# Output projection of seven query groups as seven block products in one step, and the second layer's mask held per group

## The chip, the cores and the metric

The kernel runs on one core of a Trainium2 chip. The metric is the device time of one execution in microseconds (us), lower is better. The profile is one execution taken by the hardware profiler; its times count from the first instruction. The engines are named as in the profile: PE (matrix multiply; PEld is its weight load), DVE (vector), ACT (scalar, activation functions), POOL (GpSimd) and SP (which issues most DMAs). PE writes to PSUM, the small accumulation memory, which DVE and ACT read[...]; everything else lies in SBUF.

## The reference

Two graph layers, each added to its input and normalised, on 4096 nodes with 512 features. The first is a graph attention with 4 heads over a given 0/1 adjacency. The second, which is where the change lies, is a masked attention with 8 heads of width 64:

```python
adj = jnp.maximum(adjacency_matrix, eye)
q = jnp.einsum('nd,hdk->hnk', node_matrix, Wqs)
k = jnp.einsum('nd,hdk->hnk', node_matrix, Wks)
v = jnp.einsum('nd,hdk->hnk', node_matrix, Wvs)
scores = jnp.einsum('hqk,hmk->hqm', q, k) * kd ** (-0.5)
scores = scores + IDENTITY_BIAS * eye - MASK_VAL * (1.0 - adj)
att = jax.nn.softmax(scores, axis=-1)
return jnp.einsum('hqm,hmk,hko->qo', att, v, Wo)
...
x = _layernorm(x + _L1_gnn_ref(...), axis=-1)
```

All inputs and the output are float32. The last einsum contains the output projection: the heads' outputs side by side, 4096 x 512, times Wo, 512 x 512.

## The kernel before

The first layer and the products for q, k and v fill the first 1455 us or so. They already use block products of the kind that the change brings to the output projection: a 2 x 2 blocking in which seven products of sums of blocks stand for eight (`of_weights`, `of_features`, `order`, `gemm`).

The second layer's attention follows, to the end. Queries are cut into NG = 8 groups `g` of G = 512; heads go in four pairs `m` (0 to 3). One (g, m) is called a pair here; there are 32, in the order of `pairs`. In a pair, the keys are walked in 32 tiles `j` of 128; (g, m, j) is a unit. For each unit:

- `score` (L1067): PE multiplies k and q into a PSUM tile `s_ps` of 128 keys x 2 heads x 512 queries. The pool `ps` has three such tiles, used in turn.
- `weigh` (L1281, L1284): ACT takes the exponential in place; DVE multiplies it with the mask (`keep`) into an SBUF tile `p1`, of which there are 18. The mask is float8; the 4 key tiles that hold the group's diagonal use `mdt` instead, a float32 copy made by ACT (L1044) whose diagonal POOL sets (`affine_select`, L1046).
- `add_up`: the sums over keys that the softmax divides by. Two neighbouring `p1` tiles are added by a DMA that POOL issues (L1314) and that accumulates; POOL then adds the result to `q_sum` (L1304). Two of sixteen times POOL adds both tiles itself.
- `products` (L1329): PE multiplies v and `p1` and accumulates over the 32 units in the PSUM tile `o1_ps`.

The order is written out by hand; every engine works through its instructions in program order. `step` takes a batch of NB = 3 units. It issues the scores of the batch, then its weighing and adding up, and then the products of the batch before. A pair has eleven steps, numbered 0 to 10 in this text; the last has only two units, and takes in what is left over: the row sums of the pair before (`half_sums`, L1348), and from the sixth pair on the projection of one tile of 128 queries of the group before (`project`, L1393). Both use a third `s_ps` tile, `extra`. `Later` keeps small work for later steps: `later.at(n, fn)` runs `fn` at the end of the n-th step, the current one counted as the first. So `divide` puts off the reciprocals (DVE, L1371), their spreading (ACT, L1363) and the multiplication that gives `on`, the normalised attention output of the pair (POOL, L1367, six steps on).

`project` multiplies `on` of four head pairs with `wo_sb`, four matmuls of 128 x 128 with 128 x 512. In the profile every float32 matmul shows as two records. `close1` (L1403) adds the residual `y`, which `load_y` brought, and takes the mean and variance (`normal_factors`: DVE, then four small POOL operations); four steps later ACT normalises and SP stores the rows. Four pairs of a group thus carry the four tiles of the group before. After the last pair a tail does what is left: DVE adds up the last `p1` tiles (L1461), PE projects the last five tiles, and so on.

SP loads k and v in chunks of CH = 8 key tiles, one chunk ahead (`loads`, `load_kv`), q per pair, and the mask: `load_adjT` (L1034) takes 4 key tiles x W = 1024 queries, so two groups, as it lies in DRAM (4096 bytes a partition); eleven such tiles of 4 KB a partition are kept, and the next two groups' mask is loaded during m = 3 of every second group. The spare room for sums of blocks in the q, k and v products (`spare`) comes from the same tiles.

## Time and profile before

| what | value |
|---|---|
| time, median of 3 runs | 3380.09 us (3379.16 to 3389.31) |
| the profiled execution, first to last instruction (span) | 3376.2 us |
| PE busy | 3351.0 us, 99% of the span |
| DVE busy | 2405.8 us, 71% |
| ACT busy | 1991.2 us, 59% |
| POOL busy | 2244.8 us, 66% (95% or more in the second layer's attention) |
| DMA engines, mean rate | 184 GB/s |

The three run times are of unprofiled executions; of the profiled one only the span is known. A matmul's record is longer than the time for which it keeps the next one waiting, since matmuls are pipelined, so times on PE are read from start to start. A line such as "x24 ... 2.75" merges 24 records in a row. An engine's idle time ahead of an instruction is given in brackets with what ended it.

### The profile page before, as it was taken

What the parts mean: (1) busy time and instruction counts of PE and PEld (TensorE: products, weight loads), DVE (VectorE), ACT (ScalarE), POOL (GpSimd) and SP (SyncE); (2) the same over time, 40 slices, a digit from 0 to 9 for tenths busy, and PEclk for the clock granted to TensorE, in tenths of its full rate; (3) what the DMA queues carried; (4) which work ended last, traced back from release to release, by engine and by line L of the source; (5) the groups of instructions that cost most, each with busy time, mean ns of one, the idle gap of its engine ahead of it and who ended that gap; (6) DMA issues with size and microseconds to landing.
All of it is one profiled execution on the core that took longest, in us unless ns stands there. A gap on an engine that the chain in (4) does not pass through costs nothing.

```text
span 3376.2 us, 66035 instructions
## 1 busy us (share of the span) xinstructions
PE 3351.0 (99%) x26970; PEld 1921.4 (57%) x26970; DVE 2405.8 (71%) x2485; ACT 1991.2 (59%) x2468; POOL 2244.8 (66%) x1592
## 2 busy tenths in 40 slices
PE   9999999999999999999999999999999999999998
PEld 5669999999999855543333333333333333333332
DVE  6889899998898721157766767666676666667676
ACT  1347877878876421156665656656566656656564
POOL 5650021030030174569999999999999999999996
PEclk9999999999999999999999999999999999999999
DMA  7989979769451263388989898899989889898884
GB/s 192 202 157 159 183 195 213 172 141 210 132 163 64 42 210 111 115 223 193 211 193 223 223 212 194 201 207 233 215 190 211 195 199 254 192 211 192 205 198 111
DMA packets 397129, 620.36 MB, mean 184 GB/s; under 512 B 165520, under 2 KB 242576, under 8 KB 395792
## 3 DMA queue, kind: packets, MB, share of 16 engines
q0 software_dynamic: 97376, 258.50, 42.2%
q1 hardware_dynamic: 298912, 356.49, 35.4%
q8 instruction: 214, 3.51, 0.4%
q10 hardware_dynamic: 528, 1.05, 0.1%
q14 instruction: 99, 0.81, 0.1%
HBM read 315.87 MB, written 117.64 MB: 128 GB/s over the span
## 4 chain that ended last, share of the span: by engine, by line
PE 97%; DVE 1%; DMA 1%; ACT 0%; POOL 0%; issue 0%; SPq 0%; POOLq 0%; DVEq 0%
PE o_ps L1016 27%; PE o_ps L1329 26%; PE s_ps L1067 26%; PE s_ps L1132 5%; PE s_ps L1393 3%; PE o_ps L877 3%; PE s_ps L1125 3%; PE o_ps L818 2%; DMA wq<-in_L_gnn_Wqs_dram 1%; PE s_ps L1348 1%; PE o_ps L871 0%; PE x_ps L997 0%; PE x_ps L735 0%; DVE p L1461 0%; PE x_ps L1125 0%; DVE x_sb L784 0%
## 5 line engine op out<-in xcount | busy, mean ns | idle before, releaser
L1304 POOL TENSOR_TENSOR q_sum<-q_sum,p 128x1024 f32<-128x1024 f32 x538 | 1375.8, 2557 | 62.2 <-DMA p<-p 39.0
L1284 DVE TENSOR_TENSOR p<-s_ps,adjT 128x1024 f32<-128x1024 f32 x896 | 1043.7, 1216 | 466.2 <-ACT s_ps L1281 443.4
L1281 ACT ACTIVATE s_ps<-s_ps 128x1024 f32<-128x1024 f32 x1021 | 967.1, 1006 | 594.5 <-PE s_ps L1067 594.3
L1329 PE MATMUL o_ps<-p,v_sb 64*64 64x512 f32 x8192 | 943.6, 590 | 0.0
L1067 PE MATMUL s_ps<-q_sb,k_sb 64*64 64x512 f32 x8192 | 942.7, 589 | 0.0
L1016 PE MATMUL o_ps<-sup_t,p 128*128 128x129 f32 x8192 | 922.3, 275 | 3.9 <-DVE p L633 3.9
L1016 PEld LDWEIGHTS o_ps<-sup_t,p 128*128 128x128 f32 x8192 | 919.7, 192 | 4.9 <-DVE p L633 3.9
L633 DVE SCALAR_TENSOR_TENSOR p<-fr_t,dj,az 128x1024 f32<-128x1024 f32 x512 | 654.6, 1288 | 80.9 <-PE o_ps L1016 53.5
L1329 PEld LDWEIGHTS o_ps<-p,v_sb 64*64 64x64 f32 x8192 | 310.3, 133 | 570.6 <-issue 560.3
L1067 PEld LDWEIGHTS s_ps<-q_sb,k_sb 64*64 64x64 f32 x8192 | 312.8, 133 | 565.9 <-issue 457.0
L624 ACT ACTIVATE z<-fr_t,f 128x1024 fp8e4<-128x1024 f32 x512 | 558.0, 1144 | 120.1 <-DVE az L628 119.7
L1314 POOL DMA_DIRECT2D p<-p x412 | 438.3, 1303 | 10.0 <-PE o_ps L1329 8.4
L980 POOL DMA_DIRECT2D agg<-base_d x32 | 28.6, 1201 | 526.8 <-ACT agg L967 526.6
L1284 DVE TENSOR_TENSOR p<-s_ps,md 128x1024 f32<-128x1024 f32 x128 | 150.5, 1217 | 67.3 <-ACT s_ps L1281 63.4
L628 DVE TENSOR_TENSOR az<-adjT,z 128x512 int32<-128x512 int32 x256 | 176.0, 688 | 4.1 <-ACT z L624 3.4
L584 POOL COPY seen<-token 128x1 f32<-128x1 f32 x24 | 14.0, 582 | 240.1 <-DVE token L582 240.1
L1139 ACT ACTIVATE sb<-s_ps 128x1024 f32<-128x1024 f32 x35 | 35.8, 1024 | 188.6 <-PE s_ps L1132 125.9
L597 ACT ACTIVATE adjT<-stage 128x1024 fp8e4<-128x1024 bf16 x128 | 130.9, 1050 | 4.5 <-DMA stage<-adj_d 4.5
L1154 POOL TENSOR_TENSOR sb<-sb,sb 128x1024 f32<-128x1024 f32 x36 | 84.4, 2359 | 71.7 <-ACT sb L1139 71.7
L877 PE MATMUL o_ps<-pw_sb,xT 128*128 128x512 f32 x256 | 115.1, 592 | 0.0
L1178 DVE COPY k_sb<-s_ps 128x1024 f32<-128x1024 f32 x12 | 14.7, 1224 | 139.2 <-PE s_ps L1132 89.5
L1393 PE MATMUL s_ps<-wo_sb,on 128*128 128x512 f32 x240 | 110.8, 604 | 0.0
(164 smaller groups left out, 2171.7 us busy)
## 6 DMA issues: line engine op xcount, KB each, us to landing
p<-p POOLq DMA_DIRECT2D x412, 512.0 KB, 9.1
k_sb<-k_d SPq DMA_DIRECT2D x128, 512.0 KB, 8.0
v_sb<-v_d SPq DMA_DIRECT2D x128, 512.0 KB, 5.9
adj_d<-in_adj_dram POOLq DMA_DIRECT2D x32, 1024.0 KB, 12.3
sup_t<-sup_d SPq DMA_DIRECT2D x120, 258.0 KB, 7.3
fr_t<-fr_d SPq DMA_DIRECT2D x16, 1024.0 KB, 7.5
adjT_d<-adjT SPq DMA_DIRECT2D x32, 512.0 KB, 4.5
adjT<-adjT_d SPq DMA_DIRECT2D x32, 512.0 KB, 6.7
```

Of the source, the lines that this page charges most:

```text
L624: nc.scalar.activation(z[:, k, :], fr[:, 0, :], AF.Sign, bias=fs[j // GT][:, 0, (j + k) % GT, h:h + 1], saturate=False)
L628: nc.vector.tensor_tensor(az.bitcast(I32), adjT[w, j // CJ][:, j % CJ:j % CJ + 2, :].bitcast(I32), z.bitcast(I32), op=ALU.bitwise_and)
L633: nc.vector.scalar_tensor_tensor(p, fr[:, 1, :], dj[j // GT][:, j % GT, h:h + 1], az_t[w, h, j // 2][:, j % 2, :], op0=ALU.max, op1=ALU.mult)
L877: nc.tensor.matmul(b_ps, xT[:, c, t * P:(t + 1) * P], pw_sb[c], start=(c == 0), stop=(c == KC - 1))
L1016: nc.tensor.matmul(o[t // BK][:, t % BK, :], p[:, t * P:(t + 1) * P], s, start=(j == 0 and t % BK == 0), stop=(j == NT - 1), skip_group_ch ...
L1067: nc.tensor.matmul(s[c:c + MS, e, :], k[r, a + c:a + c + MS], qt[g, m][r, :], start=True, stop=True)
L1281: nc.scalar.activation(s, s, AF.Exp)
L1284: nc.vector.tensor_tensor(p, s, keep[:, None, :].to_broadcast([P, HP, G]), op=ALU.mult)
L1304: nc.gpsimd.tensor_tensor(q, q, p, op=ALU.add)
L1314: later.at(2, lambda: nc.gpsimd.dma_start(a, b, accum_op=ALU.add))
L1329: nc.tensor.matmul(o[c, n, :], v[r, j % CH, c], p[r, e, :], start=(j == 0), stop=(j == NT - 1))
L1393: nc.tensor.matmul(s, on_t[g][:, m, t * P:(t + 1) * P], wo_sb[:, m, :], start=(m == 0), stop=(m == NP1 - 1))
```

## The change

The projection of groups 0 to 6 no longer goes tile by tile. For each of them, one extra step in the pair (g + 1, 1) projects all 512 queries at once. `on` (512 queries x 512) and `wo` (512 x 512) are cut into 2 x 2 blocks of 256 x 256, and the result is built from seven products of blocks or sums of blocks instead of eight, in four PSUM banks; each product is four matmuls of 128 x 128 with 128 x 256. The last group is still projected tile by tile in the tail.

```diff
+            def combine_wo(i):
+                a, b = {5: (wo_block(0, 1), wo_block(0, 0)), 6: (wo_block(1, 1), wo_s[5]),
+                        7: (wo_block(1, 1), wo_block(0, 1)), 4: (wo_block(1, 0), wo_s[6])}[i]
+                nc.vector.tensor_tensor(wo_block(0, 1) if i == 7 else wo_s[i], a, b,
+                                        op=ALU.subtract)
...
+            def combine_on(g, i):
...
+                a, b, op = {5: (on_block(g, 1, 0), on_block(g, 1, 1), ALU.add),
+                            6: (on_s[5], on_block(g, 0, 0), ALU.subtract),
+                            7: (on_block(g, 0, 0), on_block(g, 1, 0), ALU.subtract),
+                            3: (on_block(g, 0, 1), on_s[6], ALU.subtract)}[i]
+                nc.vector.tensor_tensor(on_block(g, 1, 0) if i == 7 else on_s[i], a, b, op=op)
+
+            def project_group(g):
+                ts = [ps.tile([P, HP, G], F32, name="s_ps") for _ in range(2)]
...
+                def add(dst, src):
+                    nc.vector.tensor_tensor(dst, dst, src, op=ALU.add)
+
+                for i in (1, 5, 2, 6, 7, 3, 4):
+                    more = i in (2, 3, 4)
+                    for t in range(2):
+                        for c in range(2):
+                            nc.tensor.matmul(bank[i][:, t, :], a[i][:, c, t * P:(t + 1) * P],
+                                             b[i][:, c, :], start=not more and t == 0 and c == 0,
+                                             stop=c == 1, skip_group_check=True)
+                    if i == 1:
+                        nc.scalar.activation(u, bank[1], AF.Copy)
+                    elif i == 6:
+                        add(u, bank[6])
+                    else:
+                        add(y[{5: (1, 1), 2: (0, 0), 7: (1, 1), 3: (0, 1), 4: (1, 0)}[i]], bank[i])
+
+                add(y[0, 1], u)
+                for m in range(2):
+                    later.at(1, lambda m=m: add(y[1, m], u))
+                for t in range(GT):
+                    later.at(2 + t, lambda t=t: close1(g, t))
```

Products 2, 3 and 4 accumulate in the banks of 1, 5 and 7. The four sums of `wo` are made once, on DVE, one every second step from the end of step 8 of the second pair on; the fourth block is overwritten in place, and `load_wo_again` brings it back after pair (7, 1) for the last group. The four sums of `on` are made on DVE for each group.

The steps of a pair with a block are cut otherwise, twelve instead of eleven: eight of three units, then one unit (step 8, which has the block), three, two (with the row sums) and two. Two sums of `on` are issued ahead of step 6 and two ahead of step 7, before those steps' own work; the residual's two tiles (four DMAs) ahead of step 0:

```diff
+            with_block = cut([NB] * (n_full - 2) + [1, NB, 2, 2])
...
+                    if block is not None and k == 0:
+                        for i in range(2):
+                            load_y(block, i)
+                    if block is not None and k in (n_full - 4, n_full - 3):
+                        for i in ((5, 6), (7, 3))[k - n_full + 4]:
+                            combine_on(block, i)
```

In `step`, `project_group` stands after the weighing of the step's unit and before the products of the step before.

The mask is kept per group, in six tiles of 8 key tiles x 512 queries (4 KB a partition), each filled by two DMAs with runs of 512 bytes, and loaded during m = 3 of every group at key tiles 0, 12 and 20. The room for sums of blocks in the q, k and v products gets tiles of its own, except for three that still come from the mask's:

```diff
-        def load_adjT(w, c):
-            at[w, c] = lp.tile([P, CJ, W], F8, name="adjT1", bufs=NCJ + 3)
-            nc.sync.dma_start(at[w, c], adjT_d[w][c])
+        def load_mask(g, c):
+            at[g, c] = lp.tile([P, CH, G], F8, name="mask", bufs=NCH + 2)
+            r = g * G % W
+            for k in range(CH // CJ):
+                nc.sync.dma_start(at[g, c][:, k * CJ:(k + 1) * CJ, :],
+                                  adjT_d[g * G // W][c * CH // CJ + k][:, :, r:r + G])
...
-                if m == NP1 - 1 and (g + 1) * G % W == 0 and g + 1 < NG and j % CJ == 0:
-                    for c in ((0, 1) if j == 0 else (j // CJ + 1,) if j // CJ + 1 < NCJ else ()):
-                        load_adjT((g + 1) * G // W, c)
+                if m == NP1 - 1 and g + 1 < NG:
+                    for c in {0: (0, 1), CH + CJ: (2,), 2 * CH + CJ: (3,)}.get(j, ()):
+                        load_mask(g + 1, c)
```

## The prediction

> **What bounds the kernel now.** I read the page first: busy shares, then the chain that ended last (97% PE). Then the windows by pair, the PE timeline of one pair, and DVE and POOL beside it.
>
> ```profile
> PE 3351.0 (99%) x26970; PEld 1921.4 (57%) x26970; DVE 2405.8 (71%) x2485; ACT 1991.2 (59%) x2468; POOL 2244.8 (66%) x1592
> ```
>
> The windows (span; PE, PEld, DVE, ACT, POOL; clock, DMA share, GB/s) of a pair without and one with a projection:
>
> ```profile
> 1620.66:1676.32 55.66, 55.66 (x524) 19.63 (x521) 39.39 (x35) 37.10 (x50) 55.03 (x37) 1.00 0.88 202
> 1787.65:1846.94 59.29, 59.29 (x532) 21.07 (x528) 41.03 (x38) 35.79 (x47) 54.95 (x36) 1.00 0.87 209
> ```
>
> PE is never idle in layer 1, so PE work taken out is time taken out, and anything that makes PE wait is time put in. POOL is nearly full too: 55.03 of 55.66.
>
> PE, first around a projection, then in a plain step (start, length, count):
>
> ```profile
> 2200.88 1.90 PE L1067 MATMUL s_ps<-q_sb,k_sb 64*64 64x512 f32 x16
> 2202.71 0.64 PE L1348 MATMUL s_ps<-q_sum,ones 128*32 128x256 f32 x8
> 2203.28 3.70 PE L1393 MATMUL s_ps<-wo_sb,on 128*128 128x512 f32 x8
> 2206.91 2.81 PE L1329 MATMUL o_ps<-p,v_sb 64*64 64x512 f32 x24
> ...
> 2229.27 2.75 PE L1067 MATMUL s_ps<-q_sb,k_sb 64*64 64x512 f32 x24
> 2231.85 2.75 PE L1329 MATMUL o_ps<-p,v_sb 64*64 64x512 f32 x24
> 2234.42 2.75 PE L1067 MATMUL s_ps<-q_sb,k_sb 64*64 64x512 f32 x24
> ```
>
> A projected tile occupies PE for 2206.91 - 2203.28 = 3.63 us; the two windows differ by the same 3.63. A plain step lasts 5.15: three scores (A, B, C, 0.86 each) and three products.
>
> Matmuls with 256 columns, as the change uses, stand in the v product:
>
> ```profile
> 1438.09 7.07 PE L1125 MATMUL s_ps<-wv,adjT 128*128 128x256 f32 x32
> 1444.99 3.62 PE L1125 MATMUL s_ps<-wv_s,xT 128*128 128x256 f32 x16
> ```
>
> 32 records take 6.90 us: 0.2156 each.
>
> DVE in a pair without projection, then POOL beside it:
>
> ```profile
> 1706.62 3.49 DVE L1284 TENSOR_TENSOR p<-s_ps,adjT 128x1024 f32<-128x1024 f32 x3 [1.66 <-ACT s_ps L1281]
> 1711.70 3.49 DVE L1284 TENSOR_TENSOR p<-s_ps,adjT 128x1024 f32<-128x1024 f32 x3 [1.59 <-ACT s_ps L1281]
> 1716.85 3.49 DVE L1284 TENSOR_TENSOR p<-s_ps,adjT 128x1024 f32<-128x1024 f32 x3 [1.66 <-ACT s_ps L1281]
> ```
>
> ```profile
> 1707.13 3.36 POOL L1304 TENSOR_TENSOR q_sum<-q_sum,p 128x1024 f32<-128x1024 f32 x1
> 1710.79 2.36 POOL L1304 TENSOR_TENSOR q_sum<-q_sum,p 128x1024 f32<-128x1024 f32 x1 [0.30 <-DMA p<-p]
> 1713.10 0.86 POOL L1314 DMA_DIRECT2D p<-p  x1
> 1714.58 4.79 POOL L1304 TENSOR_TENSOR q_sum<-q_sum,p 128x1024 f32<-128x1024 f32 x2 [0.62 <-DMA p<-p]
> 1719.32 0.86 POOL L1314 DMA_DIRECT2D p<-p  x1
> 1719.92 7.54 POOL L1304 TENSOR_TENSOR q_sum<-q_sum,p 128x1024 f32<-128x1024 f32 x3
> ```
>
> DVE is idle 1.66 us a step; POOL reads SBUF almost all the time, 2.36 us an add. DVE additions whose inputs both lie in SBUF (minimum/median/maximum ns), and the POOL addition beside the first:
>
> ```profile
> L784 DVE TENSOR_TENSOR p<-xT x30: 716/1532/1759, 42.3 to 186.6; 128x512 f32<-128x512 f32 x30
> L853 POOL TENSOR_TENSOR x_sb<-x_sb,bb x32: 1260/1713/1717, 16.9 to 217.1; 128x512 f32<-128x512 f32 x32
> L1461 DVE TENSOR_TENSOR p<-p,p x5: 1225/1226/3253, 3339.7 to 3347.2; 128x1024 f32<-128x1024 f32 x5
> ```
>
> **What the Trainium skill says.** "SBUF — State Buffer", section "Who interferes with whom": a DVE instruction with two SBUF inputs contends with a GpSimd instruction that reads SBUF; under "SBUF: two separate sides", the shared port pair is an exclusive lock, and the later one waits for the whole instruction. The trace agrees: L784 takes 0.72 us alone and 1.53 to 1.76 beside POOL additions, which stretch from 1.26 to 1.71; the L1461 that met POOL's last adds took 3.25 instead of 1.23. Additions with one PSUM input do not suffer (L1403, 687 ns beside a busy POOL). "TensorE: Matmul & The Clock Gate", "Wait — 56ns, not 53.3ns?": a fixed 2.5 ns or so per matmul beside the columns. Here 24 matmuls of 512 columns take 10.30 us (1400.30 to 1410.60), 429.2 ns each, and 2 x 215.6 - 429.2 = 2 ns, so halving the width costs nothing. "DMA: Bandwidth & Descriptors", "Specifications": line rate from 512 B on. The mask's new runs are just that; x1T_d stores (512 B runs, 256 KB) landed in 2.7 us, base_d stores (2 KB runs) in 2.8.
>
> **The change part by part**, against the profiled span of 3376.2 us; the median, 3380.09, is 3.9 above it, and I carry that difference over.
>
> *Removed.* 28 projected tiles. The last of them stood in the tail, where PE waits for DVE's L1461 anyway (0.27 us idle at 3348.45 even with it): 0. The other 27: 27 x 3.63 = 98.0.
>
> *Added on PE.* Seven blocks of 28 matmuls, 56 records: 56 x 0.2156 = 12.07, plus 0.16 to change tile shape on entry (1455.45 + 2.57 to 1458.18) and 0.20 on leaving (3.63 less 8 x 0.429): 12.43. Times 7: 87.0. **PE alone: -11.0.**
>
> *Inside the block.* Product 2 adds onto the bank that ACT copies after product 1; product 5 (1.72 us) covers the copy (0.60 by L1445). Products 3 and 4 reuse banks that DVE has read, each with 1.72 us of cover for 0.69 (L1403). Uncovered, 0.9 each; I take 0. After product 4, three products (2.57) cover the release of the bank.
>
> *The four combinations of on.* Two DVE additions before step 6's weighing, two before step 7's, all SBUF with SBUF. Their source is POOL's L1367, which ended 1706.4 in the pair above, 3.7 us before step 5's weighing ended (1710.1): no wait for data. Queued behind them on DVE is the step's weighing; behind that wait PE's next scores, which reuse its PSUM tiles. The slack: A's score ends 2230.13, its weighing starts 2231.49 and ends 1.21 later, 2.57 after the score; PE wants A's tile at 4.29. Spare: 1.72 for A, 1.44 for B (1.14 a weighing against 0.86 a score), 1.17 for C; DVE's own idle 1.66 comes first. Running them through the rows above: the first waits for the add ending 1710.5 and ends 1711.0; the second, behind the next add, 1713.75. Weighing starts at 1713.8, 2.1 late; C's tile is 0.95 late, and PE with it. Step 6's weighing ends 1717.2; the third waits for the second add of 1714.58 (to 1719.3), ends 1719.8; the fourth slips in before the next add, 1720.5. Step 7's weighing is 3.65 late; PE wants its A and B tiles in step 8 and is 2.3 late in all. If POOL happened to be waiting for a DMA each time: 4 x 0.68, absorbed, 0. If each waits for a whole add (2.36 + 0.49): near 5 us a pair, 3.3 then 6.7 late, less 1.44: 5.2. I take 2.3: **7 x 2.3 = +16.1**.
>
> *The three additions of u.* After the block, also SBUF with SBUF. POOL by then has done what it can: its next add waits for a DMA issued at about 1728 (9.1 us to land), while these start at 1736. Cover: step 9's weighing can't start before products (2.57 + 0.2), a score (0.86) and an exp (1.0), some 5 us after the block, against 0.7 + 3 x 0.7. I take 0; with one POOL add in between about 1, with three 4.
>
> *The cut 1, 3, 2, 2.* In step 9 three scores are followed by only one product: A's tile is wanted 1.72 + 0.86 = 2.58 after its score and ready at 2.57; B at 3.44 against 3.71; C, for the row sum, 0.3 later still: about 0.6. **7 x 0.6 = +4.2.** The four closings (0.87 on DVE, one a step) fit into the 1.66.
>
> *The mask.* 64 loads of 256 KB for 32 of 512 KB, all issued by SP; a chunk waits for a weighing long past and comes 15 us before use, so the k and v loads queued behind it on SP keep their lead. In its pair the DMA needs 2.1 MB beside 202 GB/s x 55.66 us = 11.2 MB, 240 GB/s; a pair with 248 GB/s lost no PE time (1846.94 to 1906.20). 0, a few us if landings of p<-p slip. Four loads of y at step 0 are wanted 45 us later: 0.
>
> *POOL.* In the pair with the diagonal, 18 adds x 2.36, L1367 2.25, 13 issues x 0.6 (1719.32 to 1719.92) and four selects of 0.9 make 56.1, a little over 55.66; DVE already waited 1.7 for q_sum there. The next pair recovers it: +2 in all (0 to 12). Start of the layer (tiles move; second weighing now waits for POOL) and four combinations of wo, one every second step: +1 (0 to 3).
>
> Sum: -11.0 + 16.1 + 4.2 + 2 + 1 = +12.3: span 3388.5, **median 3392.4**, 0.36% slower. A measurement here tells 0.3%, or 10.1 us.
>
> **Rivals.** (1) *The locks miss*: POOL waits for its DMAs when DVE asks, only the short step costs. For: at 2241.6 POOL idled 2.26 us. Against: adds and L1367 fill 45 of 55.66 us. -11.0 + 4.2 + 1 = -5.8: 3374.3, no difference; it decides from under 2.6 us of stall a group down. With the short step absorbed too, 3369, faster. (2) *Every combination meets a whole add*: 5.2 + 0.6 + 1 = 6.8 a group: -11.0 + 47.6 + 3 = 3420. For: L784's median is the contended one. Against: a fifth of POOL's time is issuing. (3) *POOL becomes the bound* once three pairs of four last 55.66, and the 1.7 us for which DVE waits in each diagonal pair are no longer covered: 3392.4 + 7 x 1.7 = 3404. Against: the plain pairs from 1565 to 1788 ran at 55.66 each.
>
> **How the numbers follow.** Likeliest case 0.50, with its own range 3384 to 3402 (stall 1.7 to 4.3 a group); (1) 0.20; (2) 0.18; (3) 0.12. The range, 3372 to 3418, leaves out a tenth on either side. Faster: 0.08, from (1) with nothing lost. Same: the rest of (1), 0.12, and two fifths of the likeliest: 0.32. Slower: 0.60.
>
> **What would show it.** Plain pairs of 55.66 in the first three of each group; the block 12.4 us with no wait inside; the new DVE additions of on at 1.5 us mean or more instead of 0.68, and PE score loads waiting for DVE before the block, 2.3 us a group. Means near 0.7 speak for (1), 2.5 for (2); weighing that waits on q_sum, for (3). Block products that wait for DVE or ACT would make the whole sum wrong.

## The result and the profile after

The changed kernel takes 3459.24 us (median of four runs, 3449.92 to 3463.36), the kernel before, beside it on the same chip, 3382.02 (median of four, 3379.16 to 3389.31): a ratio of 1.0222, 95% interval 1.0209 to 1.0236. It is slower, as forecast, but by 77 us instead of 12, and far outside the range. The profiled execution has a span of 3453.9 us against 3376.2, so 77.7 us have to be found.

The page's busy times and, from the chain of work that ended last, its shares by engine:

```profile
PE 3366.9 (97%) x27138; PEld 1948.7 (56%) x27138; DVE 2479.9 (72%) x2552; ACT 1995.7 (58%) x2475; POOL 2245.3 (65%) x1592
...
PE 67%; POOL 11%; issue 9%; DMA 7%; DVE 5%; ACT 1%; SPq 0%; POOLq 0%; DVEq 0%; ACTq 0%
```

Before, PE carried 97% of that chain. Now a third of it runs through POOL, DVE, transfers and issuing: PE waits. (PE's busy time is up by 16 us although its work is down; PE's records cover part of its waiting, so its idle time is read from start to start.)

The windows of three successive pairs, from one row sum to the next (length; PE, PEld, DVE, ACT, POOL busy; clock, DMA share, GB/s). The first holds the block of group 0, the second is the pair behind it, the third a plain one:

```profile
1738.87:1810.59 71.72, 66.79 (x549) 28.04 (x545) 51.44 (x47) 34.25 (x45) 57.22 (x33) 1.00 0.77 175
1810.59:1874.24 63.65, 60.90 (x552) 20.67 (x552) 44.86 (x45) 39.59 (x51) 57.05 (x48) 0.97 0.73 186
1874.24:1929.90 55.66, 55.66 (x524) 19.64 (x520) 39.39 (x35) 37.10 (x50) 54.57 (x36) 1.00 0.94 225
```

The third pair has the 55.66 us that were expected of every plain pair. The block pair has 71.72, and POOL, which has no idle time to give away in a plain pair (54.57 of 55.66), stands idle for 14.5 us in it. The pair behind has 63.65. Over the layer the four pairs of a group have these means, counted from the block pair: 70.59, 63.04, 55.66, 57.69, together 247.0, where before four pairs of 59.29 make 237.2. The cut of the steps moves two units of scores and products (2 x 1.715 = 3.43 us) from the block pair to the one behind.

So the 77.7 us go like this, on the terms of the prediction:

| term | forecast | measured | how read |
|---|---|---|---|
| tile projections out, seven blocks in | -11.0 | -12 | 27 x 3.63 less 7 x 12.28 (a block without a wait, e8 below) |
| waits inside a block | 0 | 23 | six blocks last 15.45, one 16.76, each less 12.28 |
| the sums of on | 16.1 | 16 | block pair 70.59, without the sums 68.27 (below): 2.3 x 7 |
| the short step | 4.2 | 4 | 68.27 - (55.66 - 3.43 + 15.45) = 0.59, x 7 |
| behind the block ("POOL") | 2 | 40 | 63.04 - 55.66 - 3.43 = 3.95, x 7; 57.69 - 55.66 = 2.03, x 6 |
| start of the layer | 1 | 7 | first row sum at 1571.88, before at 1564.99 |

The six rows add up to 78. The price of the sums of on is a mean of unequal groups: the seven block pairs last 71.72, 68.27, 73.03, 70.48, 70.26, 68.27 and 72.11 us, so two groups lost nothing by them and one 4.8 us.

Two terms were missed by 20 us and more, and each has its own picture. The first is the block on PE (start, length, count; in brackets the wait ahead and what ended it):

```profile
1785.69 1.09 PE L1069 MATMUL s_ps<-q_sb,k_sb 64*64 64x512 f32 x8 [1.80 <-DVE p L1286]
1786.82 1.99 PE L1458 MATMUL s_ps<-wo_sb,on 128*128 128x256 f32 x8
1789.50 1.99 PE L1458 MATMUL s_ps<-wo_s,on_s 128*128 128x256 f32 x8 [0.69 <-ACT u_sb L1462]
1792.43 1.97 PE L1458 MATMUL s_ps<-wo_sb,on 128*128 128x256 f32 x8 [0.93 <-DVE y L1452]
1794.23 1.89 PE L1458 MATMUL s_ps<-wo_s,on_s 128*128 128x256 f32 x8
1796.90 1.99 PE L1458 MATMUL s_ps<-wo_sb,on 128*128 128x256 f32 x8 [0.78 <-DVE u_sb L1452]
...
1802.28 2.81 PE L1331 MATMUL o_ps<-p,v_sb 64*64 64x512 f32 x24
```

1802.28 - 1786.82 = 15.46 us, and the next five blocks last 15.45. The waits are at product 5 (for ACT's copy of product 1), at product 2 (for DVE's reading of product 5) and at product 7 (for DVE's reading of product 6). None of these three shares a bank with the product whose reader it waits for. They share a *tile*: banks 1 and 5 are the halves of one `s_ps` tile, 6 and 7 those of the other, and the program's waits are set for a whole tile.

The second is POOL behind the block:

```profile
1794.83 1.19 POOL L1316 DMA_DIRECT2D p<-p  x1
1804.56 0.85 POOL L1316 DMA_DIRECT2D p<-p  x1 [8.54 <-PE o_ps L1331]
1805.12 2.67 POOL L1306 TENSOR_TENSOR q_sum<-q_sum,p 128x1024 f32<-128x1024 f32 x1
1811.44 0.23 POOL L511 TENSOR_SCALAR bn_ve<-bn_mv 128x1 f32<-128x1 f32 x1 [3.65 <-DVE bn_mv L509]
```

It waits 8.54 us for products of PE that stand behind the block (3.5 to 11.4 us behind the seven blocks, 6.6 on average; it ends 2.3 us behind the block each time), and then 3.65 us more, in its own queue, for the statistics of a closing that DVE hasn't reached. Further down the same pair its transfers come late, and DVE's weighing, which needs the `p` tiles that they release, waits, and then PE for the weighing. DVE, then PE:

```profile
1861.18 2.35 DVE L1286 TENSOR_TENSOR p<-s_ps,mask 128x1024 f32<-128x1024 f32 x2 [3.72 <-DMA p<-p]
```

```profile
1862.46 1.98 PE L1069 MATMUL s_ps<-q_sb,k_sb 64*64 64x512 f32 x8 [2.75 <-DVE p L1286]
```

The same link over the whole run, from the lists of waits (total, times, longest), before and then after:

```profile
DVE p L1284 <- DMA p<-p: 6.7, 13, 1.3
```

```profile
DVE p L1286 <- DMA p<-p: 58.3, 38, 3.9
```

Last the sums of on, as DVE ran them in the first block pair:

```profile
1772.58 1.43 DVE L1433 TENSOR_TENSOR on_s<-on 128x512 f32<-128x512 f32 x1
1774.04 2.74 DVE L1433 TENSOR_TENSOR on_s<-on_s,on 128x512 f32<-128x512 f32 x1
1776.70 3.47 DVE L1286 TENSOR_TENSOR p<-s_ps,mask 128x1024 f32<-128x1024 f32 x3
1780.10 1.65 DVE L1433 TENSOR_TENSOR on<-on 128x512 f32<-128x512 f32 x1
1781.67 2.83 DVE L1433 TENSOR_TENSOR on_s<-on,on_s 128x512 f32<-128x512 f32 x1
```

All 28 of them take 48.4 us, 1.73 on average, where one that meets no addition of POOL's takes 0.68.

### The profile page after: what moved, and what is told of

Read it like the earlier page. It is cut to its first block, busy times and chain, and to the rows that moved or that the text cites. A ratio compares the mean times of both kernels' runs of the same rounds, so it can differ in the third digit from the quotient of the medians.

```text
span 3453.9 us, 66600 instructions
## 1 busy us (share of the span) xinstructions
PE 3366.9 (97%) x27138; PEld 1948.7 (56%) x27138; DVE 2479.9 (72%) x2552; ACT 1995.7 (58%) x2475; POOL 2245.3 (65%) x1592
## 4 chain that ended last, share of the span: by engine, by line
PE 67%; POOL 11%; issue 9%; DMA 7%; DVE 5%; ACT 1%; SPq 0%; POOLq 0%; DVEq 0%; ACTq 0%
PE o_ps L1016 20%; PE o_ps L1331 15%; PE s_ps L1069 15%; DMA p<-p 7%; POOL q_sum L1306 6%; PE s_ps L1135 5%; PE o_ps L877 3%; PE s_ps L1128 3%; PE s_ps L1458 2%; PE o_ps L818 2%; DVE p L1286 2%; POOL p L1316 2%; POOL bn_rs L513 1%; DVE on_s L1433 0%; POOL q_sum L1302 0%
## 5 line engine op out<-in xcount | busy, mean ns | idle before, releaser
L1286 DVE TENSOR_TENSOR p<-s_ps,mask 128x1024 f32<-128x1024 f32 x896 | 1045.1, 1216 | 437.4 <-ACT s_ps L1283 359.3
L1069 PE MATMUL s_ps<-q_sb,k_sb 64*64 64x512 f32 x8192 | 956.4, 592 | 39.8 <-DVE p L1286 39.1
L1331 PE MATMUL o_ps<-p,v_sb 64*64 64x512 f32 x8192 | 953.6, 594 | 0.0
L1316 POOL DMA_DIRECT2D p<-p x412 | 432.4, 1299 | 61.8 <-PE o_ps L1331 60.9
L1157 POOL TENSOR_TENSOR sb<-sb,sb 128x1024 f32<-128x1024 f32 x36 | 84.4, 2357 | 71.7 <-ACT sb L1142 71.7
L1365 ACT ACTIVATE r<-r_h 32x256 f32<-32x256 f32 x248 | 102.2, 412 | 2.9
```

The source lines that it names most:

```text
L1069: nc.tensor.matmul(s[c:c + MS, e, :], k[r, a + c:a + c + MS], qt[g, m][r, :], start=True, stop=True)
L1286: nc.vector.tensor_tensor(p, s, keep[:, None, :].to_broadcast([P, HP, G]), op=ALU.mult)
L1316: later.at(2, lambda: nc.gpsimd.dma_start(a, b, accum_op=ALU.add))
L1331: nc.tensor.matmul(o[c, n, :], v[r, j % CH, c], p[r, e, :], start=(j == 0), stop=(j == NT - 1))
```

## The experiments

All times below are medians, each ratio is to the kernel before, run beside it on the same chip; "against the changed kernel" is against 3459.2, whose own four runs spread over 13 us, so a smaller difference is read from the traces. A group's length is the sum of the mean lengths of its four pairs; POOL's and DVE's busy times per group are means over the six groups from the fourth row sum on.

**First theory: the order of the work makes PE and POOL wait in and at the block.** The block's products wait for readers of a neighbour bank, the sums of on hold up the weighing, and POOL waits for products of PE that stand behind the block. Each of the first four expectations names its rivals; the chief one, their "second theory", is the mask, now held in runs of 512 bytes, which would slow every transfer; their "third" is that the sums of on make everything behind them late.

*e1: the block's products in an order in which neighbours lie in different tiles.*

```diff
-                for i in (1, 5, 2, 6, 7, 3, 4):
+                for i in (1, 6, 2, 7, 5, 4, 3):
```

> The block's products in the order 1, 6, 2, 7, 5, 4, 3, so that neighbours lie in different PSUM tiles; nothing else. First theory (four causes side by side: products that wait for the reader of the neighbouring bank of their tile, 3.2 us a block; DVE sums of on that wait for POOL's adds; POOL held up because the products of step 7 stand behind the block on PE; moved tiles at the start): each block falls from 15.45 to about 12.3 us, total 15 to 30 us less than the changed kernel's 3459. Second theory (the mask's 512-byte runs slow the DMAs and late p<-p landings do all the rest): the waits in the block are only a sign of it, total less than 10 us lower. Third theory (the locked sums of on make everything late): the same, less than 10 us lower.

3435.32 us, ratio 1.0158 (1.0131 to 1.0185): 24 us less. The first block on PE:

```profile
1800.17 1.99 PE L1458 MATMUL s_ps<-wo_sb,on 128*128 128x256 f32 x8
1802.10 1.99 PE L1458 MATMUL s_ps<-wo_s,on_s 128*128 128x256 f32 x8
1803.93 3.62 PE L1458 MATMUL s_ps<-wo_sb,on 128*128 128x256 f32 x16
...
1812.65 2.81 PE L1331 MATMUL o_ps<-p,v_sb 64*64 64x512 f32 x24
```

No wait is left, and the block lasts 12.48 us; the seven last 12.28 to 13.97, with one wait of 0.40 us in one of them. The waits inside the block are shown to be those of the tile. (This profiled execution began its attention loop 16 us late, which its span of 3452.6 holds and the median doesn't; its groups are read here, not its span.)

*e2: the products of the step before ahead of the block, so that POOL's work isn't behind it.*

```diff
-                if block is not None:
-                    project_group(block)
...
                 for g, m, j in last:
                     products(g, m, j)
+                if block is not None:
+                    project_group(block)
```

> In the step with the block, the products of the step before are issued ahead of the block instead of behind it; nothing else. First theory: POOL's wait for PE's o_ps (60.9 us in 12 times) falls below 20, DVE's wait for p<-p (58 us) below 20, the pair after the block falls from 63.0 to about 59 (55.66 and the 3.4 that the cut moves over), total 25 to 45 us less than 3459, less about 1 us a group because the release of the block's tiles is no longer covered. Second and third theory: POOL's wait goes, but the total stays within 8 us.

3456.12 us, 1.0221 (1.0181 to 1.026): nothing gained. POOL's wait for PE fell from 60.9 us in all to 13.0, but another took its place:

```profile
1807.10 0.23 POOL L511 TENSOR_SCALAR bn_ve<-bn_mv 128x1 f32<-128x1 f32 x1 [7.38 <-DVE bn_mv L509]
```

POOL went ahead to the closing and stood there. The pair behind the block kept its length (62.84). That part of the theory fell in this form: to take one of two waits in a row away gains nothing.

*e3: no sums of on.* Left out: the four combinations; the block uses plain blocks of on in their place.

```diff
-                    if block is not None and k in (n_full - 4, n_full - 3):
-                        for i in ((5, 6), (7, 3))[k - n_full + 4]:
-                            combine_on(block, i)
```

> The four sums of on are left out and the block uses plain blocks of on in their place, so the result of groups 0 to 6 is not the reference's; this shows the price of the sums. First theory: 15 to 35 us less than 3459 (3.3 us of PE time ahead of the block a group, and a little of what follows). Third theory: 60 to 80 us less, about the time of the kernel before. Second theory: 15 to 25 us less.

3440.85 us, 1.0172 (1.0146 to 1.0198): 18 us less. The seven block pairs are now equal to 0.02 us; the first:

```profile
1739.93:1808.20 68.27, 65.79 (x549) 28.43 (x546) 43.32 (x43) 34.06 (x45) 60.11 (x36) 1.00 0.84 193
```

Hence the sums cost 70.59 - 68.27 = 2.3 us a group. The pair behind stays at 63.1, although POOL's wait behind the block is only 2.6 to 3.8 us here: it ends at the same place, 2.3 us behind the block, so the loss of the pair behind doesn't follow from the length of this wait alone. The third of the expected cases (60 to 80 us) fell; the other two had forecast the same range here.

*e4: the kernel before with the mask of the change (loads per group, its tiles, the spare room), and its tile-by-tile projection.*

```diff
-                    for c in ((0, 1) if j == 0 else (j // CJ + 1,) if j // CJ + 1 < NCJ else ()):
-                        load_adjT((g + 1) * G // W, c)
+                    for c in {0: (0, 1), CH + CJ: (2,), 2 * CH + CJ: (3,)}.get(j, ()):
+                        load_mask(g + 1, c)
```

> The kernel before with the mask held per group and the room for sums moved as in the change, but its own projection tile by tile. First theory: 0 to 10 us above the kernel before (3382), all of it at the layer's start. Second theory: 40 to 70 us above. Third theory: within 3 us.

3382.95 us, 1.0006 (0.9996 to 1.0016), and pairs of 59.29 us as before. The mask costs nothing that can be measured here; that rival fell.

**Second theory (A): POOL is the bound behind the block.** A plain pair leaves it 1 to 2% of slack, so what it loses in a block it could not make up. Rival (B): POOL only follows.

*e5: two of POOL's additions left out early in the pair behind a block.*

```diff
-                    later.at(5, lambda: add(a))
+                    if not (m == 2 and g and i in (2, 3)):
+                        later.at(5, lambda: add(a))
```

> Left out: in the pair after each block pair (groups 1 to 7), two of POOL's additions to the sum of p (5 us of POOL in a pair), so the divisors of those pairs are too small. Theory A (after a block POOL is the bound: in the block it has no p to add, and what it loses there comes on top of pairs that need it for 97% of their time): that pair falls from 63.0 to 58.0 us or below and the pair behind it from 57.7 to about 56, so the time falls by 30 to 45 us against the changed kernel, to 3415 to 3430, ratio to before 1.010 to 1.015. Theory B (the stalls after a block are of the weighing or of the products alone and POOL only follows): within 8 us of the changed kernel, 1.020 to 1.024.

3457.56 us, 1.0247 (1.0197 to 1.0298): no gain. The pair behind fell to 60.49, and the third pair rose from 55.66 to 59.68. POOL was busy 4.2 us less in a group (221.1 against 225.4) and idle 4.2 us more (25.4 against 21.2).

*e6: the four closings of a group nine steps apart.*

```diff
-                    later.at(2 + t, lambda t=t: close1(g, t))
+                    later.at(2 + 9 * t, lambda t=t: close1(g, t))
```

> The four closings of a group's rows (1.25 us of POOL each) nine steps apart instead of one; nothing is left out. Theory A: POOL's surplus of 3.7 us in the pair after the block goes, that pair falls by 2.5 to 4 us and the pair behind it by up to 2, the time by 15 to 35 us, ratio 1.012 to 1.018. Theory B: within 8 us of the changed kernel.

3466.47 us, 1.0244 (1.0224 to 1.0265): no gain. The windows of the pair behind a block and the next:

```profile
1808.44:1867.78 59.34, 59.34 (x552) 20.66 (x553) 43.30 (x41) 37.38 (x48) 51.55 (x37) 1.00 0.66 153
1867.78:1930.66 62.88, 59.35 (x524) 19.82 (x520) 40.16 (x37) 38.57 (x52) 61.80 (x44) 0.95 1.03 251
```

The pair behind loses nothing now (55.66 + 3.43 + 0.25), but POOL stands idle for 7.8 us in it and has 61.8 us of work in the next, which pays. POOL's wait for the statistics grew from 70.7 us to 93.8: a closing by itself costs a stand of its own. In both runs the loss moved and kept its size. Theory A as I put it, that less work on POOL would do, fell.

*e7: the tiles of wo_s allocated at their first use, behind the first `p1` tiles.*

```diff
-            wo_s = {i: wp.tile([P, 2, D // 2], F32, name=f"wo_s{i}", bufs=1) for i in (5, 6, 4)}
+            wo_s = {}
...
             def combine_wo(i):
+                if i == 5:
+                    wo_s.update({k: wp.tile([P, 2, D // 2], F32, name=f"wo_s{k}", bufs=1)
+                                 for k in (5, 6, 4)})
```

> The three tiles of wo_s are allocated when the first difference of wo is made, behind the first p, instead of ahead of them; nothing is left out. If the 5.6 us that the changed kernel loses at the start of the attention loop (the second weighing waits 6.1 us for a k tile that POOL evicts) come from where the p tiles lie, the time falls by 4 to 6 us, the groups' periods stay as they are, ratio 1.020 to 1.021. If they come from something else of the change (the mask, the differences of wo themselves), nothing moves.

3450.88 us, 1.0209 (1.0192 to 1.0226): 8 us less, which is within the spread of the runs, but the first row sum stands at 1566.1 instead of 1571.9. DVE's second batch of weighing, in the changed kernel and then here:

```profile
1466.33 3.49 DVE L1286 TENSOR_TENSOR p<-s_ps,md 128x1024 f32<-128x1024 f32 x3 [6.11 <-POOL k_sb L1157]
```

```profile
1465.11 1.23 DVE L1286 TENSOR_TENSOR p<-s_ps,md 128x1024 f32<-128x1024 f32 x1 [2.84 <-ACT s_ps L1283]
```

Three small tiles ahead of the `p1` tiles in the pool move these on to memory that POOL's last operation of the q, k and v products, on a tile named `k_sb`, still used. That is 5.8 of the 6.9 us lost at the start.

*e8: the edits of e1, e6 and e7 together, and the sums of on one in each of four steps, with the block one step later.*

```diff
-            with_block = cut([NB] * (n_full - 2) + [1, NB, 2, 2])
+            with_block = cut([NB] * (n_full - 1) + [1, 2, 2])
...
-                    if block is not None and k in (n_full - 4, n_full - 3):
-                        for i in ((5, 6), (7, 3))[k - n_full + 4]:
-                            combine_on(block, i)
+                    if block is not None and n_full - 4 <= k < n_full:
+                        combine_on(block, (5, 6, 7, 3)[k - n_full + 4])
```

> Together: block products in the order 1,6,2,7,5,4,3, the sums of on one in each of four steps with the block one step later, the closings nine steps apart, wo_s allocated later; nothing is left out. Theory A: the savings of the single edits add up, 24 by the order, 10 to 15 of the 18 by the sums, 15 to 35 by the closings, 5 by the start: 3380 to 3405, ratio 0.999 to 1.007. Theory B (POOL isn't the bound): only order and sums count, 3415 to 3430, ratio 1.010 to 1.015.

3430.35 us, 1.0149 (1.013 to 1.0167), groups of 242.7. All seven blocks last 12.28 or 12.29: with the sums and the order mended, nothing waits inside a block. The gain is 29 us, little more than the order's alone, and what the second of the two expectations had; the closings gave nothing, as in e6. The block pairs still last 70.2 us on average, where the shortest has 66.39, and DVE's wait for `p` has grown to 105.0 us, half of it in these pairs.

**Third theory (C): it is POOL's standing idle, not its work.** POOL takes its instructions in order. While it stands at the head of its queue for PE or for DVE, additions that could run wait behind it; since a plain pair leaves it 1 us, PE pays later. Work taken from where POOL would have stood anyway (e5) only lengthens the stand.

*e9: POOL's four small operations of a closing issued two steps after DVE's statistics.*

```diff
+        def rest():
             nc.gpsimd.tensor_scalar(ve, mv[:, 1:2], EPS, None, op0=ALU.add)
             nc.gpsimd.tensor_tensor(rs, ve, minus_half, op=ALU.pow)
             nc.gpsimd.tensor_tensor(nb, mv[:, 0:1], rs, op=ALU.mult)
             nc.gpsimd.tensor_scalar(nb, nb, -1.0, None, op0=ALU.mult)
+        at(2, rest)
```

> POOL's four small operations of each closing are issued two steps after VectorE's statistics, so POOL doesn't stand in its queue for them; nothing is left out. Theory C (POOL has 1 to 2% of slack in a plain pair, so each time it stands idle, in the block for PE and behind the block 3.7 us for the statistics, is a debt that it can't work off, and PE pays it in one of the next pairs): the 3.7 us go in each group, 15 to 30 us in all, ratio 1.013 to 1.018. If the debt is made in the block alone: within 8 us of the changed kernel.

3449.91 us, 1.0215 (1.0192 to 1.0237): 9 us less, short of the 15 to 30 and within the spread of the runs. POOL's idle time fell by 3.6 us a group, as expected, the group by 1.9. The pair behind has 60.84, the third and fourth 56.24 and 58.02.

*e10: two additions left out late in each of the two pairs behind a block pair.*

```diff
-                    later.at(5, lambda: add(a))
+                    if not (g and m in (2, 3) and i in (9, 12)):
+                        later.at(5, lambda: add(a))
```

> Left out: two additions to the sum of p late in each of the two plain pairs behind a block pair (four a group, 9.4 us of POOL), so those pairs' divisors are too small. Theory C: unlike the two additions left out early in the pair, where POOL was idle anyway (it only waited longer there), these pay off the debt: the fourth pair comes back to 55.7 us and the next block pair to 68.3, the time falls by 25 to 45 us, ratio 1.009 to 1.015. If POOL isn't what PE waits for: within 8 us of the changed kernel.

3459.2 us, 1.024 (1.0217 to 1.0263): no gain in time, though half of what was expected did happen. A block pair, the pair behind and the other two:

```profile
1983.34:2056.97 73.63, 67.98 (x548) 28.59 (x544) 51.89 (x47) 34.24 (x45) 56.61 (x33) 0.98 0.74 167
2056.97:2120.27 63.30, 61.28 (x553) 20.89 (x553) 44.88 (x45) 39.53 (x51) 56.86 (x48) 0.97 0.74 187
2120.27:2175.93 55.66, 55.66 (x524) 19.64 (x520) 39.40 (x35) 37.10 (x50) 52.36 (x36) 1.00 0.99 234
2175.93:2231.59 55.66, 55.66 (x524) 19.64 (x520) 39.40 (x35) 35.01 (x46) 51.34 (x32) 1.00 0.93 224
```

The fourth pair is back at 55.66 in every group (57.69 in the changed kernel), so what it lost was POOL's lag. But the block pair didn't come to 68.3; it rose to 71.7 on average, and POOL stands idle in the one above for 17.0 us. Most of the rise stands ahead of the block, on PE:

```profile
2030.71 1.98 PE L1069 MATMUL s_ps<-q_sb,k_sb 64*64 64x512 f32 x8 [3.09 <-DVE p L1286]
```

The weighing came late because the four sums of on ahead of it took 0.68, 2.74, 2.52 and 3.26 us: POOL was adding nearly all the while, and three of them met its additions. So a POOL that was on time gained nothing here: the sums met it more often (8.2 us for the four in these six block pairs, 6.9 in the changed kernel), and in the block it had nothing to do.

*e11: e8, and of a closing only the power stays on POOL, two steps behind the statistics; DVE does the other three.*

```diff
-        nc.gpsimd.tensor_scalar(ve, mv[:, 1:2], EPS, None, op0=ALU.add)
+        nc.vector.tensor_scalar(ve, mv[:, 1:2], EPS, None, op0=ALU.add)
...
+        def power():
+            nc.gpsimd.tensor_tensor(rs, ve, minus_half, op=ALU.pow)
...
+        def shift():
+            nc.vector.tensor_tensor(nb, mv[:, 0:1], rs, op=ALU.mult)
+            nc.vector.tensor_scalar(nb, nb, -1.0, None, op0=ALU.mult)
+        at(2, power)
+        at(3, shift)
```

> The four edits together, and of each closing only the power stays on POOL (0.6 of 1.25 us), two steps behind the statistics; nothing is left out. Theory C: POOL has 2.6 us less to do in a group and stands idle some 7 us less; against the four edits alone (1.0149) 20 to 40 us less, ratio 1.003 to 1.009. If POOL isn't the bound: 1.013 to 1.016.

3438.54 us, 1.0165 (1.0148 to 1.0182), far from what was expected and on its face 8 us worse than e8. The trace says otherwise: its groups last 238.0 us against 242.7, and its first row sum stands at 1611.6 instead of 1567.4. The edit sits in a function that the first layer calls too, where DVE now waited for POOL's powers; from the list of waits:

```profile
DVE bn_nb L520 <- POOL bn_rs L517: 43.0, 40, 5.3
```

*e12: e11, and two of a pair's 18 additions moved from POOL to DVE.*

```diff
                 elif i % 8 == 7:
-                    later.at(2, lambda: add(a))
-                    later.at(3, lambda: add(b))
+                    later.at(3, lambda: nc.vector.tensor_tensor(a, a, b, op=ALU.add))
+                    later.at(4, lambda: add(a))
```

> As the run before, and two of the 18 additions of a pair go from POOL to VectorE (the two that are made without an accumulating transfer: VectorE adds one p to the other, POOL adds the result); nothing is left out. POOL then needs 50 of the 55.7 us of a plain pair, VectorE 43. Theory C: the debt is worked off inside a pair, periods of 55.7 us everywhere but in the block pair, 3365 to 3385, ratio 0.996 to 1.001. Against it: VectorE's additions meet POOL's (2 to 3 us each instead of 1.2) and the weighing comes late: over 1.003.

3470.99 us, 1.025 (1.0225 to 1.0275). Groups of 240.9 against 238.0: POOL's load fell by 16 us a group, DVE's rose by 16, and POOL's waits for PE grew from 62.4 to 158.4 us in all. DVE never waits for `p` any more, so the lag is gone; but PE's waits for DVE's weighing grew from 8.8 to 16.6 us, as the expectation's second case had it. A lighter POOL is no cure if the weighing is later for it. (Its first row sum stands at 1623.5, later still than in e11, so its total says little on theory C; its groups do.)

*e13: e11 with the first layer as it was.*

```diff
+        if at is None:
+            nc.gpsimd.tensor_scalar(ve, mv[:, 1:2], EPS, None, op0=ALU.add)
+            nc.gpsimd.tensor_tensor(rs, ve, minus_half, op=ALU.pow)
+            nc.gpsimd.tensor_tensor(nb, mv[:, 0:1], rs, op=ALU.mult)
+            nc.gpsimd.tensor_scalar(nb, nb, -1.0, None, op0=ALU.mult)
+            return rs, nb
```

> The four edits and the closings with only the power on POOL, as the run two before, but in the second layer alone: there the same edit also stood in the first layer, where VectorE then waited 43 us for POOL's powers and the attention loop began 44 us later (1611.6 against 1567.4), while a group took 238.0 us against 242.7 with the four edits alone. Theory C (each time POOL stands idle is a debt that PE pays): a group of 238 us and a start at 1567, 3390 to 3398, ratio 1.003 to 1.005. If the late start had made the groups short: 242 us a group, 1.012 or above.

3391.25 us, 1.0031 (1.0021 to 1.0041), as expected: 68 us of the 77 are gone with nothing left out of the computation. POOL around the end of the second block:

```profile
2030.07 3.32 POOL L1320 TENSOR_TENSOR q_sum<-q_sum,p 128x1024 f32<-128x1024 f32 x1
2035.41 0.87 POOL L1330 DMA_DIRECT2D p<-p  x1 [2.03 <-PE o_ps L1345]
```

POOL's stand behind the seven blocks is 1.7 to 2.6 us instead of 3.5 to 11.4, there is none at the closing (one of 3.4 us stands later in the pair), and DVE's wait for `p` is down to 11.0 us in all. Groups last 237.3. The block pair and the one behind:

```profile
1971.94:2038.44 66.50, 66.50 (x564) 29.21 (x560) 50.94 (x46) 33.78 (x45) 60.10 (x36) 1.00 0.88 207
2038.44:2096.57 58.13, 57.81 (x540) 19.94 (x536) 44.39 (x46) 37.39 (x49) 53.58 (x35) 1.00 0.79 187
```

*e14: e13, and the products ahead of the block as in e2.*

> As e13, and the products of the step before are issued ahead of the block, so POOL doesn't wait for them through the block. Theory C: unlike on the changed kernel alone, where the wait for the statistics took its place, POOL now works through the block; one to two us a group less than e13: 3378 to 3390, ratio 0.999 to 1.003. If what is left of the loss lies in the block and the sums of on: as e13, 1.003 to 1.005.

3429.7 us, 1.0158 (1.0128 to 1.0187): 38 us worse than e13, the opposite of what was expected. The loss lies in the pair behind the block, which lasts 63.9 us instead of 58.1. DVE and PE there, behind the second block:

```profile
2043.17 6.21 DVE L1469 TENSOR_TENSOR y<-y,u_sb 128x512 f32<-128x512 f32 x3
```

```profile
2050.57 3.69 PE L1083 MATMUL s_ps<-q_sb,k_sb 64*64 64x512 f32 x16 [4.69 <-DVE p L1300]
```

POOL does work through the block now, without an idle moment, and so it meets the three additions of u, both of whose inputs lie in SBUF: they take 4.4 to 6.3 us behind the seven blocks. The weighing of the next step stands behind them, and PE, which has the products of only one unit left behind the block, waits for it 2.9 to 4.8 us each time. In e13 they take 4.4 us too, but there the products of three units stand behind the block and PE waits 0.3. POOL does wait 7.2 to 8.1 us for products a little later, but these are products that PE does behind its own wait. My expectation was wrong, and so was its mechanism: the edit took away what covered PE while DVE was busy. PE's waits for the weighing are 34.1 us in the whole run, 8.4 in e13.

*e15: the kernel before with one more addition on POOL in each pair of groups 1 to 7* (a sum of two p is added twice).

```diff
                     later.at(5, lambda: add(a))
+                    if g and i == 8:
+                        later.at(5, lambda: add(a))
```

> The kernel before with one more addition on POOL in each pair of groups 1 to 7 (one sum of two p is added twice, so the divisors are too large): POOL then needs some 58.7 of the 59.3 us of a pair, the 97 to 99% that it needs of a plain pair in the changed kernel. Theory C: PE begins to wait in the kernel before too, by 0.5 to 1.5 us a pair: 12 to 40 us more, ratio 1.004 to 1.012. If POOL's load isn't what PE waits for: within 3 us, 0.999 to 1.001.

3424.17 us, 1.0122 (1.0103 to 1.0141): 43 us for 28 additions of 2.36, a little above the 12 to 40 expected; each would have been free if POOL had had room. The same wait as in the changed kernel appears, here in a kernel without any block:

```profile
DVE p L1284 <- DMA p<-p: 76.0, 52, 3.0
```

*e16: e14 with one addition late in each pair of groups 1 to 7 left out.*

```diff
-                    later.at(5, lambda: add(a))
+                    if not (g and i == 12):
+                        later.at(5, lambda: add(a))
```

> As e14, and one addition late in each pair of groups 1 to 7 left out (2.4 of POOL's 54 us in a pair; the divisors are too small). Theory C with a debt that is still there in e14: 5 to 15 us less than e14. If e14 has no debt left and the rest is the block: within 4 us of e14.

3380.65 us, 0.9998 (0.9988 to 1.0009): 49 us less than e14, for 27 additions of 2.36 (64 us of POOL; the last pair has its own end), far more than the 5 to 15 expected, and the kernel before's time with one addition of each pair left out. Most of that is not a debt paid off, though. Some 37 of the 49 us lie in the pair behind the block (58.7 us instead of 63.9): the addition that is left out falls due about the block, POOL is all but done when DVE comes to the three additions of u, these take 1.9 to 3.7 us and PE waits 0.4 to 2.2 for the weighing behind them. So of this pair of runs only e15 shows what POOL's room in a pair is worth.

*Two tries at a version that beats the kernel before, both from e13. e17: the multiplication that gives on moves from POOL to DVE. e18: one of the two places where POOL adds two p itself uses an accumulating transfer.*

```diff
-                    nc.gpsimd.tensor_tensor(on_t[g][:, m, :], o_sb.pop((g, m)), r, op=ALU.mult)
+                    nc.vector.tensor_tensor(on_t[g][:, m, :], o_sb.pop((g, m)), r, op=ALU.mult)
```

```diff
-                elif i % 8 == 7:
+                elif i % 16 == 15:
```

> As e13, and the multiplication of o by the reciprocals (1.2 to 1.9 us of POOL in a pair) goes to VectorE; nothing is left out. Theory C: POOL's slack in a plain pair doubles; the 6.8 us that the groups of e13 take longer than those of before go, and up to 10 more: 3372 to 3385, ratio 0.997 to 1.001. If VectorE's operation meets POOL's additions and holds up the weighing: 1.003 to 1.008.

> As e13, and one of the two places in a pair where POOL adds two p itself uses an accumulating transfer as the others do: 1.5 us less of POOL (2.4 less one issue of 0.9), 0.5 MB more to move, in each pair; nothing is left out. Theory C with POOL alone as the limit: 3372 to 3385, ratio 0.997 to 1.001. If the DMA engines (0.9 to 0.97 of a plain pair) are the next limit: 1.003 or above.

e17: 3388.0 us, 1.0015 (1.0007 to 1.0023), groups of 237.6, as in e13; POOL has 5 us a group less to do and DVE some 3 more. It is the best version found, and 0.15% slower than the kernel before, just short of what was expected. e18: 3417.37 us, 1.0115 (1.0098 to 1.0132): one transfer more in a pair costs 26 us. POOL's waits for PE grew to 122.6 us (50.7 in e13), and a p transfer lands after 10.3 us instead of 9.8. The plain pairs lose nothing; the block pairs last up to 73.9 us, and in five of them PE waits for a load of k, 17.0 us in all. SP and PE in the second block pair:

```profile
1973.31 1.22 SPq L1068 DMA_DIRECT2D k_sb<-k_d  x1
```

```profile
1995.64 1.69 PE L1083 MATMUL s_ps<-q_sb,k_sb 64*64 64x512 f32 x8 [3.42 <-DMA k_sb<-k_d]
```

The load was issued behind the four of y and landed 22 us later, where the median of this run's loads of k is 8.1 us. So most of the loss is one of transfers, as the expectation's second case had it; why just these loads are so late was not followed up.

## Why the prediction was wrong

**Right.** PE alone (-11.0): a plain pair without a wait has 55.66, a block without waits 12.28. The sums of on: I took 2.3 us of PE's time a group from the rows of the trace, and the pair periods of e3 give 2.3; the mechanism (a DVE operation with two inputs in SBUF waits for a whole addition of POOL's, as the Trainium skill's "SBUF — State Buffer", section "Who interferes with whom", has it) shows in 1.73 us on average against 0.68. That the mean came out so well is in part luck: the price runs from nothing to 4.8 us, by where POOL's additions happen to fall. The short step: 0.6 taken, 0.59 measured. The additions of u: three in 1.89 us, no contention, as argued; once POOL works on through the block they take 4.4 (e13) to 6.3 us (e14), and PE waited up to 4.8 for what stood behind them; the prediction had put that case at 1 to 4. The mask: nothing (e4).

**Wrong, first step: "Inside the block ... Uncovered, 0.9 each; I take 0".** I counted the cover per bank: the next product runs in another bank while the last one is read. The program's waits go by tile, and two banks are one tile. So product 5, which I had as the cover for ACT's copy, waited for it, and products 2 and 7 waited for DVE. The measured size is 3.2 us a block, 23 us in all, a little over three times the uncovered 0.9. The prediction's last sentence had named this as what would make the sum wrong; the order in the diff and the lines that allocate the banks would have told.

**Wrong, second step: "POOL ... +2 in all (0 to 12)".** This is the largest miss, 40 us. I had summed POOL's work in a pair against the pair's length, found 56.1 against 55.66 in the worst pair and let the next recover it. What the sum leaves out is that POOL stands idle at fixed places: 3.5 to 11.4 us behind a block, since its transfers need products that PE does after it, and 3.7 us at the closing. Before, every pair had 3.63 us of projection in which POOL caught up; now three pairs in four have none, and in the block, in which POOL should have caught up, it has no work for 1.4 to 9.1 of the 15.45 us. So "the next pair recovers it" failed: the plain pairs behind a block pair lasted 63.04 - 3.43 = 59.6 and 57.7 us instead of 55.66. That PE pays for POOL's lag is shown by DVE's wait for `p` (6.7 us before, 58.3 after), which goes with the lag in e12 and e13, and by e15, where the same wait and 43 us came from more work on POOL alone. How the 40 us divide between the stand behind the block and the stand at the closing is not shown. Rival (3) had POOL as the bound, but through the diagonal pair and at 1.7 us a group; its mechanism, DVE waiting for `q_sum`, isn't what happened (12.1 us of it before, 13.0 after).

**Wrong, third step: the start, "+1 (0 to 3)".** I had seen that tiles move and that the second weighing then waits for POOL. The wait took 6.1 us, the start came 6.9 us later, and e7 gave 5.8 of them back.

**What stays open.** e9 alone gave 9 us and e8 alone 29, together with three small operations moved to DVE they gave 68; how much of that step from e8 to e13, 39 us, is the wait and how much is the load (1.0 us of POOL's busy time a group) wasn't separated. Nor is it settled what the last 10 us of e13 are (8 in its profiled execution): 3 lie ahead of the first block, the rest behind it, in single pairs of 56 to 60 us that no edit removed. There is little to be won in any case: with the shortest pairs that e13 and e17 show, 66.39, 58.07 and twice 55.66, a group would take 235.8 us against 237.2 before, an estimate of 10 us for all seven.

## What to carry to other kernels

Before work is gathered into one place, look at the engines that run beside the bound one: if one of them has 1 or 2% of room, ask where it catches up, and whether it will have work to catch up with in that place. An in-order queue has two costs, its work and its stands; taking work away where it stands gains nothing, and taking one stand away only moves it to the next instruction that isn't ready, so the whole chain of stands has to be followed. And before an operation is moved out of one engine's way, look at what it was the cover for: in e14 it freed POOL, and uncovered DVE. A stand in the trace can be the effect and not the cause, so look at what came late just ahead of it. Cover for a reader of PSUM is counted per unit on which the program sets its waits, not per bank.

## What the hardware showed beyond that

A POOL with 225.1 us of work in groups of 236.6 was free in the kernel before; with 9.4 us more a group (e15), 99% of the same 236.6, the groups came to 242.9 and the kernel lost 43 us. I had not expected the edge to be that sharp; that the 9 to 10 us which a transfer of `p` takes to land use up the lead of the 18 `p` tiles is my reading of it, and wasn't tested. The order of seven products, which changes nothing in what PE computes, was worth 24 us. And three additions on DVE of 0.68 us each, with both inputs in SBUF, took 1.9 us in the changed kernel and up to 6.3 in e14, with POOL adding at the time.
